# Local attention on one Trainium2 core: two heads in zero-padded query blocks, probabilities divided before their transposes, value products that come out transposed

## The chip, the cores and the metric

The kernel runs on one core of one Trainium2 chip. The core has five engines with a queue each: TensorE (PE in the profile; its weight loads are listed apart as PEld), VectorE (DVE), ScalarE (ACT), GpSimd (POOL) and SyncE (SP), which only issues DMAs here. PE reads its operands from SBUF and writes to PSUM, which has eight banks of 128 partitions by 512 float32 values. The metric is the device time of one execution in microseconds (us), lower is better. Times here come from a set of three runs and from one execution that the hardware profiler recorded.

## The reference

The program is a two-layer network over 16 sequences of 512 tokens with 128 features, all in float32. Layer 0 is `x + s * g`: `s` is a gated causal convolution of the normalised input, and `g` is the SiLU of a small transformer of depth 2 with local attention. Layer 1 is again `x + s * g`, with a 16-head attention and a soft mixture of experts. The change touches the local attention alone, which runs 2 x 16 times (depth times sequences), with 8 heads of 64 and a window of 64:

```python
def local_attention(q, k, v):            # q, k, v: b, h=8, n=512, d=64
    w = n // WINDOW                      # 8 windows of 64 queries
    bq = q.reshape(b, h, w, WINDOW, d) * QK_SCALE
    bk, bv = look_around(bk), look_around(bv)     # window w-1 and window w: 128 keys
    sim = einsum('bhwid,bhwjd->bhwij', bq, bk)
    mask = (i < j) | (i > j + WINDOW) | (j == -1)
    sim = where(mask, -finfo.max, sim)
    attn = softmax(sim, axis=-1)
    out = einsum('bhwij,bhwjd->bhwid', attn, bv)
...
q, k = l2norm(q) * qs, l2norm(k) * ksc
q, k = rotary_xpos(q, k)
o = local_attention(q, k, v)
x = x + o @ wo
```

So each head and window makes a 64 x 128 block of scores, a softmax along its 128 keys, and a 64 x 64 block of output.

## The kernel before

The kernel is written as Python generators, one for each stage and sequence: `conv` (the convolution), `layer(b, 0)` and `layer(b, 1)` (the two depths of the transformer, `L0` and `L0b` in the plan), `pre` (`A`: the second layer norm, projections and rotation of layer 1), `first` and `second` (`S1`, `S2`: the two passes of the 16-head attention, first the row maxima, then the exponentials and value products), and `moe` (`M`). A heap resumes the generators by planned times: every `yield` carries a weight, and a stage's position advances by its weight over the stage's total (`PLAN`, `TOT`). This decides the order in which instructions are recorded. A scheduler then reorders them on each engine by its own timing model (`TLS = True`), taking an instruction that was recorded later where an earlier one is not ready, as far as buffers allow. The order of every engine's queue is therefore fixed when the kernel is built, and on the chip each queue runs strictly in that order, apart from weight loads that PE pulls ahead.

Because several sequences are in flight at once, `L0` of one sequence, `L0b` of the one before, and `A`, `S1`, `S2` and `M` of still earlier ones share the engines. PSUM is divided among them by tags with one bank each: `sc` for scores, `x` and `y` for all other products of `L0` and `L0b`, `pq` for the projections, `a` for the small stages, and `s1`, `s2`, `pv` for the passes of layer 1. Near the end of the program the table `TAIL` lets the last sequences use the banks that have become free.

Inside `layer`, the 8 heads are taken as 4 pairs, `c` = 0 to 3. For each pair:

- `proj(c)` makes queries, keys and values of all 512 tokens (PE `pq`, lines 212 to 214), copies them out of PSUM on ACT (lines 313, 314), rotates and scales them on DVE and POOL (lines 317 to 337), and keeps the values in `vbuf` and a copy shifted by 64 tokens in `vsbuf`. Both hold 64 value columns and a 65th column of ones per head.
- `turn(c)` transposes queries and keys on PE (`qT`, `kT`, helper line 200), and ACT copies each 128 x 512 result into SBUF (lines 344, 347). Rows 0 to 63 belong to the first head of the pair, rows 64 to 127 to the second.
- `attend(c)` then works head by head (`hh`). Eight products of 64 x 64 queries with 64 x 128 keys fill one bank `sc` (line 361): windows 2p and 2p+1 of one head stand in the upper and lower half of the partitions. DVE adds the mask and finds the row minimum of the negated scores (line 371, four instructions, each with a small instruction that reads the accumulator). ACT takes four exponentials (line 373). PE transposes the four blocks (`prT`, line 200), ACT copies them out (line 376), and eight products of 64 rows of probabilities with the 65 value columns fill `po` (line 380). The 65th column holds the sum of the row, so DVE takes its reciprocal (line 387) and multiplies it in on the way out of PSUM (line 388) into `o`. When both heads are done, PE transposes `o` (`oT`, four transposes) and ACT copies the result into the tile `B` (line 391), the stationary operand of the output product (line 404).

After the four pairs come the output product, the residual, the second norm and the gated MLP (lines 404 to 443). In `second`, the four value products of one key tile (line 569) write to four groups of 32 columns of the PE array and are bound together by `behind`, a dependency that keeps their order.

A float32 product appears in the profile as two matrix instructions; a transpose and a product of the rounded type fp32r appear as one. The profile names the part of the PE array that an instruction uses, such as 64\*64 for `sc`, 128\*64 for `po`, 128\*32 for `pvd` and 128\*128 for most others.

## Time and profile before

| | |
|---|---|
| three runs | 3595.16, 3603.40, 3610.21 us; median 3603.4 us |
| profiled execution, its own time | 3609.49 us |
| span of that profile | 3607.5 us |
| mean granted TensorE clock | 0.954 |
| DMA, mean | 63 GB/s |

Span is the time from the first to the last instruction of the core. An engine's busy time is the union of the intervals of its instructions, so overlapping instructions are counted once; the mean duration beside it is that of a single instruction from its start to its end, the overlap included. For pipelined instructions the distance from start to start is therefore shorter than the mean, and it is this distance that the engine's throughput follows. Idle time of an engine is put down to what ended it: another engine's instruction, a DMA, or "issue", where nothing is seen to be waited for. The program can be cut into three stretches: up to 86 us before the first scores of the local attention; from there to the last scores at 3108.6 us; and the end, in which only the later stages of the last sequences are left.

### The profile page before, as it was taken

How to read it: one execution, taken by the hardware profiler on the slowest of the kernel's cores; microseconds unless marked ns; L12 is line 12 of the kernel's file. 1: busy time of each engine (PE TensorE's matmuls, PEld its weight loads, DVE VectorE, ACT ScalarE, POOL GpSimd, SP SyncE). 2: the span in 40 equal slices, each digit the busy share in tenths (PEclk: the TensorE clock that was granted, in tenths of full speed). 3: DMA queues.
4: the chain of work that ended last, by engine and by line, in shares of the span. 5: the costliest groups of instructions: out<-in, count | busy, mean ns of one | idle time of the engine just before them, and what ended most of it. 6: DMA issues, size and time to landing. Idle time of an engine off the chain costs nothing.

```text
span 3607.5 us, 67593 instructions
## 1 busy us (share of the span) xinstructions
PE 3246.8 (90%) x24316; PEld 2324.0 (64%) x24316; DVE 2497.6 (69%) x7065; ACT 2225.3 (62%) x5003; POOL 1677.0 (46%) x1647
## 2 busy tenths in 40 slices
PE   5899878998999999989998999999989998988886
PEld 4788656666766666767675676666767665544542
DVE  7878567677676767777776777767777766654551
ACT  1546545676666666766766676667667665655553
POOL 3234464546464554645655455454645544331310
PEclk7999979899999999999999999999999999999996
DMA  6544441211222212122211212121221211011100
GB/s 220 147 126 113 107 104 43 55 46 44 70 50 58 57 43 62 45 70 50 70 47 47 58 48 66 44 68 44 59 62 44 70 34 53 25 54 40 46 25 13
DMA packets 197723, 227.82 MB, mean 63 GB/s; under 512 B 60016, under 2 KB 125712, under 8 KB 197392
## 3 DMA queue, kind: packets, MB, share of 16 engines
q1 hardware_dynamic: 154384, 138.53, 13.5%
q0 software_dynamic: 43008, 84.97, 9.6%
q8 instruction: 195, 3.19, 0.4%
q14 instruction: 136, 1.11, 0.1%
HBM read 137.49 MB, written 56.10 MB: 54 GB/s over the span
## 4 chain that ended last, share of the span: by engine, by line
PE 52%; DVE 13%; ACT 10%; issue 4%; DMA 2%; POOL 1%; SPq 0%; POOLq 0%; DVEq 0%; ACTq 0%
PE s2d L560 6%; PE pvd L569 6%; PE s1c L533 5%; PE sc L361 5%; DVE mxc L534 3%; PE po L380 3%; ACT sd L562 3%; PE pw L404 2%; PE prT L200 2%; DVE rt L317 2%; DVE q L322 2%; PE pw L442 2%; PE ppb L665 2%; PE pslb L643 1%; PE pq L212 1%
## 5 line engine op out<-in xcount | busy, mean ns | idle before, releaser
L534 DVE TENSOR_REDUCE mxc<-s1c 128x1 f32<-128x512 f32 x1024 | 698.3, 684 | 391.5 <-PE s1c L533 385.2
L562 ACT ACTIVATE sd<-s2d 128x512 f32<-128x512 f32 x1024 | 611.7, 601 | 386.6 <-PE s2d L560 377.5
L330 POOL TENSOR_TENSOR rt<-rt,q 128x512 f32<-128x512 f32 x256 | 333.4, 1303 | 553.4 <-DVE q L322 433.3
L560 PE MATMUL s2d<-QS,KS 128*128 128x512 f32 x1024 | 494.6, 487 | 63.2 <-ACT sd L562 53.8
L533 PE MATMUL s1c<-KS,QS 128*128 128x512 f32 x1024 | 476.1, 466 | 55.5 <-DVE mxc L534 42.8
L373 ACT ACTIVATE s<-s,m 128x128 f32<-128x128 f32 x1024 | 346.4, 397 | 169.5 <-DVE m L371 168.4
L560 PEld LDWEIGHTS s2d<-QS,KS 128*128 128x128 f32 x1024 | 199.0, 195 | 348.4 <-issue 217.4
L336 POOL TENSOR_TENSOR y<-ss,mhalf 128x16 f32<-128x16 f32 x128 | 381.0, 2977 | 64.8 <-DVE ss L334 53.7
L569 PE MATMUL pvd<-sd,Vt 128*32 128x512 f32 x2048 | 286.1, 630 | 29.0 <-ACT sd L562 28.7
L361 PE MATMUL sc<-kT,qT 64*64 64x128 f32 x4096 | 302.9, 281 | 5.9 <-ACT kT L347 2.8
L371 DVE CUSTOM_DVE_ANT_0 s<-sc,maskf 128x128 f32<-128x128 f32 x1024 | 236.3, 284 | 87.8 <-PE sc L361 83.7
L533 PEld LDWEIGHTS s1c<-KS,QS 128*128 128x128 f32 x1024 | 199.6, 195 | 136.8 <-DVE mxc L534 90.0
L313 ACT COPY q<-pq 128x256 f32<-128x256 f32 x512 | 192.3, 376 | 143.9 <-PE pq L214 96.8
L361 PEld LDWEIGHTS sc<-kT,qT 64*64 64x64 f32 x4096 | 228.8, 135 | 77.8 <-issue 22.6
L337 POOL TENSOR_TENSOR rt<-rt,y 128x1024 f32<-128x1024 f32 x128 | 246.6, 1926 | 4.9
L317 DVE TENSOR_TENSOR rt<-q,rot 128x512 f32<-128x512 f32 x256 | 209.0, 820 | 49.9 <-ACT q L313 42.5
L212 PE MATMUL pq<-wq,hT 128*128 128x384 f32 x512 | 212.6, 415 | 31.9 <-ACT vbuf L314 21.5
L200 PE MATMUL prT<-step,s 128*128 128x128 f32 x1024 | 204.0, 288 | 20.3 <-ACT s L373 16.9
L322 DVE TENSOR_TENSOR q<-q,rot 128x512 f32<-128x512 f32 x256 | 216.6, 846 | 4.8 <-ACT q L313 4.7
L545 POOL DMA_DIRECT2D QS<-mxd x128 | 69.1, 541 | 312.2 <-DMA mxd<-sd 273.2
L376 ACT COPY pt<-prT 128x512 f32<-128x512 f32 x256 | 149.3, 583 | 84.2 <-PE prT L200 83.2
L380 PEld LDWEIGHTS po<-vsbuf,pt 128*64 128x64 f32 x2048 | 145.5, 141 | 83.7 <-ACT pt L376 36.7
(246 smaller groups left out, 7654.4 us busy)
## 6 DMA issues: line engine op xcount, KB each, us to landing
wq<-wqd POOLq DMA_DIRECT2D x128, 384.0 KB, 4.0
vsbuf<-vbuf SPq DMA_DIRECT2D x128, 130.0 KB
QS<-scq POOLq DMA_DIRECT2D x128, 128.0 KB, 2.6
KS<-sck POOLq DMA_DIRECT2D x128, 128.0 KB, 2.5
vsbuf<-vbuf SPq DMA_DIRECT2D x128, 97.5 KB
scq<-sa SPq DMA_DIRECT2D x96, 128.0 KB
sck<-sa SPq DMA_DIRECT2D x96, 128.0 KB
toep<-in_wpad_a_dram SPq DMA_DIRECT2D x24, 240.0 KB
```

The lines of the kernel that those rows point to most:

```text
L200: PE.transpose(pt[:, p * 128 : p * 128 + 128], src(p), ident)
L317: V.tensor_tensor(rt[:, ps].rearrange("t p (i h) d -> t p i h d", i=2), qk.rearrange("t p (i h d) -> t p i h d", i=2, h=2), rot[:, l, 0, p ...
L322: V.tensor_tensor(t2, qk.rearrange("t p (i h s d) -> t p i h s d", i=2, h=2, s=2)[:, :, :, :, ::-1, :], rot[:, l, 1, ps].rearrange("t p i ...
L330: G.tensor_tensor(rf, rf, t2.rearrange("t p i h s d -> t (p i h s d)"), ALU.add)
L336: G.tensor_tensor(y.rearrange("t p g -> t (p g)"), ssf, mhalf, ALU.pow)
L361: PE.matmul(s4[q0 : q0 + 64, u // 2, :], qT[r0 : r0 + 64, 64 * u : 64 * u + 64], kT[r0 : r0 + 64, k0 : k0 + 128] if u else kT[r0 : r0 + 64 ...
L373: S.activation(pr[:, p, :], pr[:, p, :], AF.Exp, bias=m[:, p : p + 1], scale=-1.0)
L533: PE.matmul(sc, QS[:, g // 2, qt * 128 : qt * 128 + 128], KS[:, g % 2, :], start=True, stop=True)
L534: V.tensor_reduce(mx[:, g, qt : qt + 1], sc, AX.X, ALU.max)
L560: PE.matmul(sc, KS[:, g % 2, kt * 128 : kt * 128 + 128], QS[:, g // 2, :], start=True, stop=True)
L562: S.activation(e, sc, AF.Exp, scale=ISQ8)
L569: mm = PE.matmul(pv[32 * q : 32 * q + 32, :], Vt[:, kt, 9 * hd : 9 * hd + 32], es[g], start=(kt == 0), stop=(kt == 3),)
```

## The change

The pair of heads is now handled together, and half of the windows at a time.

- `turn` no longer makes a tile `qT`. ACT copies the first head's 64 rows, and DVE the second head's 64 rows, into `qbd`: for each window a 128 x 128 block with the queries of head 0 in the upper left quarter, those of head 1 in the lower right, and zeros elsewhere. The zeros are written once at the start; there is one such tile for each of the two depths.
- `attend` runs over two halves `i` of four windows. A score block is one 128 x 128 product of `qbd` with the 128 keys of both heads, so the partitions of `sc` hold 64 queries of head 0 and 64 of head 1. Four products replace eight.
- The exponential also gives the sum of each row (`accum_out`). DVE takes the reciprocal of the four sums and multiplies the 128 x 512 probabilities by it in SBUF, before the transposes. The columns of ones go.
- In the value products the values are the stationary operand and the transposed probabilities the moving one, so the result has features in partitions and tokens in columns. It is copied straight into `oT` by ACT, 128 x 256 for each half; the tile `o` and the four transposes `oT` go.
- The helper `tied` records all but the first instruction of a group at high priority and chains them with `behind`. It is used for the value products here and, in place of the loop with `behind`, for those of `second`.
- The buffers of the tag `sd` (the exponentials and other tiles of `second`) go from 6 to 5, and those of `qT` and `o` go.

```diff
-    "sd": 6, "ond": 1,
+    "sd": 5, "ond": 1,
...
-        mask[:64, p] = m0 if p == 0 else m
-        mask[64:, p] = m
+        mask[:64, p] = mask[64:, p] = m if p else m0
...
+    def tied(steps):
+        after = None
+        for step in steps:
+            if after is None:
+                after = step()
+                continue
+            with tc.high_priority():
+                mm = step()
+            behind(mm, after)
+            after = mm
...
+        t = wk0.tile([128, 8, 128], F32, name=f"qbd{l}", bufs=1)
+        G.memset(t, 0.0)
+        qbd.append(t)
...
-            v = wk0.tile([128, 4, 2, 65], F32, name=f"vbuf{l}{i}", bufs=1)
-            vs = wk0.tile([128, 4, 2, 65], F32, name=f"vsbuf{l}{i}", bufs=1)
+            v = wk0.tile([128, 4, 2, 64], F32, name=f"vbuf{l}{i}", bufs=1)
+            vs = wk0.tile([128, 4, 2, 64], F32, name=f"vsbuf{l}{i}", bufs=1)
...
-            qT = tl([128, 512], "qT")
-            S.copy(qT, quad(lambda p: rt[:, p, 0:2, :].rearrange("t g d -> t (g d)"), "qT"))
+            qb = qbd[l]
+            pt = quad(lambda p: rt[:, p, 0:2, :].rearrange("t g d -> t (g d)"), "qT").rearrange("d (u q) -> d u q", u=8)
+            S.copy(qb[0:64, :, 0:64], pt[0:64])
+            V.tensor_copy(qb[64:128, :, 64:128], pt[64:128])
...
-            for hh in range(2):
-                r0 = 64 * hh
+            for i in range(2):
...
-                for u in range(8):
-                    q0 = 64 * (u % 2)
+                for w in range(4):
+                    u = 4 * i + w
                     k0 = 64 * max(u - 1, 0)
                     PE.matmul(
-                        s4[q0 : q0 + 64, u // 2, :],
-                        qT[r0 : r0 + 64, 64 * u : 64 * u + 64],
-                        kT[r0 : r0 + 64, k0 : k0 + 128] if u else kT[r0 : r0 + 64, None, 0:64].to_broadcast([64, 2, 64]),
+                        s4[:, w, :], qb[:, u, :],
+                        kT[:, k0 : k0 + 128] if u else kT[:, None, 0:64].to_broadcast([128, 2, 64]),
                         start=True, stop=True,
                     )
...
-                    S.activation(pr[:, p, :], pr[:, p, :], AF.Exp, bias=m[:, p : p + 1], scale=-1.0)
+                    S.activation(pr[:, w, :], pr[:, w, :], AF.Exp, bias=m[:, w : w + 1], scale=-1.0, accum_out=sm[:, w : w + 1])
+                V.reciprocal(sm, sm)
+                V.tensor_tensor(pr, pr, sm[:, :, None].to_broadcast([128, 4, 128]), ALU.mult)
...
-                po3 = pt_("po")[:, 0:260].rearrange("t (p d) -> t p d", p=4)
-                for u in range(8):
-                    PE.matmul(
-                        po3[64 * (u % 2) : 64 * (u % 2) + 64, u // 2, :],
-                        prT[:, 64 * u : 64 * u + 64],
-                        (v if u % 2 else vs)[:, u // 2, hh, :],
-                        start=True, stop=True,
+                po = pt_("po")
+                tied([
+                    partial(
+                        PE.matmul, po[64 * hh : 64 * hh + 64, 64 * w : 64 * w + 64],
+                        (v if w % 2 else vs)[:, 2 * i + w // 2, hh, :], prT[:, w, hh, :], start=True, stop=True,
                     )
-                ri = tl([128, 4], "ri")
-                V.reciprocal(ri, po3[:, :, 64])
-                V.tensor_tensor(o[:, :, hh, :], po3[:, :, 0:64], ri[:, :, None].to_broadcast([128, 4, 64]), ALU.mult)
-                yield 1
-            po = quad(lambda p: o[:, p].rearrange("t h d -> t (h d)"), "oT")
-            S.copy(oT[:, c, :], po)
-            yield 0.8
+                    for w in range(4) for hh in range(2)
+                ])
+                S.copy(oT[:, c, 256 * i : 256 * i + 256], po[:, 0:256])
+                yield 1.4
```

## The prediction

> **What bounds the kernel now.** I read the page's busy shares and granted clock first, then the busy times cut at the last local attention scores (3108.6 us), then the ends of idle time, then the timeline of single groups on PE.
>
> ```profile
> PE 3246.8 (90%) x24316; PEld 2324.0 (64%) x24316; DVE 2497.6 (69%) x7065; ACT 2225.3 (62%) x5003; POOL 1677.0 (46%) x1647
> 86.30:3108.60 3022.30, 2785.01 (x22132) 2061.47 (x22132) 2196.46 (x6341) 1958.32 (x4523) 1528.46 (x1413) 0.97 0.24 63
> 3108.60:3607.50 498.90, 412.52 (x1985) 222.98 (x1981) 237.02 (x500) 251.66 (x446) 119.69 (x191) 0.90 0.13 34
> ```
>
> In the windows (length; busy PE, PEld, DVE, ACT, POOL; clock) PE is busy 92% of the long middle, DVE 73%, ACT 65%. PE is the bound, not a sharp one: busy includes pipeline tails at each wait. In the last 499 us DVE and ACT are at half load: a few dependent streams are left, and time goes into round trips. What is left there:
>
> ```profile
> L562 ACT ACTIVATE sd<-s2d 128x512 f32<-128x512 f32 x259 | 151.1, 598 | 122.9 <-PE s2d L560 117.9 <-DMA mxd<-sd 2.0 <-issue 1.1
> L533 PE MATMUL s1c<-KS,QS 128*128 128x512 f32 x232 | 112.5, 491 | 13.5 <-DVE mxc L534 8.8 <-DMA QS<-scq 2.2 <-DVE rgb L684 0.7
> L569 PE MATMUL pvd<-sd,Vt 128*32 128x512 f32 x520 | 77.7, 673 | 12.4 <-ACT sd L562 12.3
> ```
>
> A sequence has 64 of the first two, so 4.0 and 3.6 sequences of S2 and S1 wait when the local attention ends.
>
> Single groups on PE (start, length, instructions):
>
> ```profile
> 1500.07 0.59 PE L655 MATMUL phb<-sb,wf 128*128 128x512 f32 x1
> 1500.59 0.27 PE L380 MATMUL po<-vsbuf,pt 128*64 128x65 f32 x1
> ...
> 1500.99 0.22 PE L380 MATMUL po<-vbuf,pt 128*64 128x65 f32 x1
> 1501.05 0.22 PE L380 MATMUL po<-vsbuf,pt 128*64 128x65 f32 x1
> 1501.05 0.22 PE L380 MATMUL po<-vbuf,pt 128*64 128x65 f32 x1
> 1501.20 0.38 PE L404 MATMUL pw<-wo,B 128*128 128x128 f32 x1
> 1504.42 1.72 PE L404 MATMUL pw<-wo,B 128*128 128x128 f32 x14
> 1515.32 0.60 PE L200 MATMUL oT<-step,o 128*128 128x128 f32 x4
> 1520.97 0.81 PE L483 MATMUL pya<-wl,sa 128*128 128x384 f32 x2
> 1521.70 1.09 PE L361 MATMUL sc<-kT,qT 64*64 64x128 f32 x16
> 1522.72 0.50 PE L212 MATMUL pg<-hT,w1h 128*128 128x512 f32 x1
> ```
>
> `po` runs two by two, 0.06 us apart, but 0.15 us pass from the last pair to `pw`: leaving a column-split mode costs 0.09. Entering costs as much: `phb` to `po` takes 0.52 us where a full-rate 512-column instruction needs 0.43. Transposes and 128-column instructions follow each other every 0.11 us ((0.60-0.27)/3; (1.72-0.38)/13, with a 128x128 weight load before each, so the loads hide).
>
> **The change part by part.** Counts are those of the built instruction order. My sum is against the profiled execution (3609.5 us, 2.0 around its span), which is 6 us above the median of the three runs.
>
> PE. (1) The 512 `oT` transposes go: 512 x 0.11 = 56 us. (2) The scores leave 64\*64 mode; with fewer split groups, changes of PE mode along the queue fall from 1796 to 1172: 624 x 0.095 = 59 us; at least 2 x 256 groups = 49. (3) A score group took 1.02 us from start to next start, 0.93 without its exit; eight 128\*128 instructions need 8 x 0.11 = 0.88: 256 x 0.05 = 13 us, bounds 0 and 13. (4) `po` keeps 16 instructions, 64 columns for 65, still in alternating halves: 0. Together -128 us. `tied` leaves the number of `pvd` mode changes alone (311 exits before, 313 after): 0.
>
> The Trainium skill speaks against (3): "TensorEngine Tiling (Array Packing)", When to Use Tiling, asks for row tiling where the contraction is 64 or less, and the overview counts four independent tiles of 64x64; padding to 128 gives them up. By that rule a tiled group of eight products of 2 x 0.11 us, four at a time, would take 0.44 us, and the padding would cost 256 x (0.88 - 0.44) = 113 us. The row of 16 instructions in 1.09 us shows only the column pairs overlapping, since a group uses the rows of one head; the measured row decides.
>
> DVE. The multiply by line 388 goes (107.0 us busy). The multiply of 128x512 in SBUF is new: nearest row line 317, 820 ns, also two SBUF inputs; bounds 684 (line 443, one input in PSUM) and 846 (line 322): 256 x 0.82 = 210 us. The copy of 64 rows of `qT`: no such row; partition count does not matter (line 429 takes 743 ns at 85 and at 128), so 128 x 0.684 = 88 us by line 511, bounds 594 (ACT's copy) and 743. Reciprocals stay at 256. Net +191 us (+130 to +205).
>
> The skill's "SBUF — State Buffer", on the shared port pair, says a DVE instruction with two SBUF inputs and a reading GpSimd instruction exclude each other. The trace fits partly: line 317 has 820 ns against 684 with an input in PSUM. At 684 the multiply would be 35 us cheaper.
>
> ACT. `oT`'s copy goes (75.3 us), two of 128x256 come: 256 x 0.376 (line 313) = 96 us, net +21. The row sums add 1024 accumulator reads. The only row like it is in the setup:
>
> ```profile
> 463.53 0.29 ACT L864 ACTIVATE sesq<-se 128x128 f32<-128x128 f32 x1
> 463.73 0.19 ACT L864 ACTIVATION_READ_ACCUMULATOR sesq<-se 128x1 f32 x1
> 463.82 0.29 ACT L864 ACTIVATE sesq<-se 128x128 f32<-128x128 f32 x1
> 464.02 0.19 ACT L864 ACTIVATION_READ_ACCUMULATOR sesq<-se 128x1 f32 x1
> 464.12 0.29 ACT L864 ACTIVATE sesq<-se 128x128 f32<-128x128 f32 x1
> 1710.28 1.28 ACT L373 ACTIVATE s<-s,m 128x128 f32<-128x128 f32 x4 [0.94 <-DVE m L371]
> ```
>
> Starts are 0.29 us apart with a read between, and four exponentials without reads take 1.28 us, also (1.28-0.40)/3 = 0.29 apart. Reads hide inside; I take 0.09 per group of four, 24 us; bounds 0 and 1024 x 0.186 = 190. ACT then stands near 66%.
>
> Queues and buffers. SP keeps 1061 DMA issues and POOL 512; the value shifts shrink by 1/65: 0. Two memsets on POOL at the start: 0, POOL is at 46%. `qbd` has one buffer per depth where `qT` had two, so the next pair's copies wait for the second half's scores; in the order they stand behind them anyway: 0, at worst a 0.6 us hold of ACT's queue 128 times (77 us of idle on an engine with 1000 us of it). `sd` at 5: in both orders one `s2d` stands ahead of each `pvd` group at the end, which five buffers allow: 0.
>
> New waits. First, transposes no longer begin after the first exponential: three more (3 x 0.29), the last read (0.19), a reciprocal (0.17) and the multiply (0.82) come first, about 2 us. PE's queue has, by the distances above, a median 5.7 us of other work between scores and transposes, 3.6 before, so the order makes that room; PE waited 17 us for these over the whole run, I add 25 (0 to 60). Second, DVE goes from 73% to about 82% of the middle, so `s1c`, which waited 43 us for DVE's maxima, waits longer: +25 (0 to 80). The `oT` waits go (from 300 to 3000 us; total, times, longest):
>
> ```profile
> PE s1c L533 <- DVE mxc L534: 33.0, 37, 3.7
> PE oT L200 <- DVE o L388: 13.8, 9, 3.0
> PE prT L200 <- ACT s L373: 13.2, 9, 4.4
> ```
>
> Order of the stages. After the last score group the changed order leaves 155 `s1c`, 189 `s2d` and 192 `pvd` products (before: 232, 259, 260): later stages keep pace with the local attention. The end shrinks: by `s2d` to 499 x 189/259 = 364, by `s1c` to 333; since the last sequence's own chain does not scale, I take 390 (333 to 470). The work that moves into the middle costs PE 77 x 0.23 + 70 x 0.23 + 17 groups x 1.0 = 51 us, and about 31 for the mixture and rotation rows that move along: +82.
>
> Sum: start 86.3 + 2.0 around; middle 3022.3 - 128 + 82 - 15 (`oT` idle) + 50 = 3011; end 390: 3490 us, 3.3% below the profiled 3609.5. As a cross-check, 3609.5 - 128 - 15 with all other waits kept gives 3467.
>
> **The rivals.** A difference of 0.5% (18 us) is about what a measurement of this kernel can tell from no change.
>
> - Half of it: the order's shorter end is paid back in a middle where DVE and ACT stand fuller. New waits of 130 us (nearly the sum of both upper bounds) instead of 50 give 3570; with an end of 360 instead of 390, 3540. For it: 82% on DVE; against: most DVE idle time is waiting for PE.
> - PE's time was not what held it: the removed work turns into idle, and the end does not shrink: 3600. Against: idle on PE in the middle is only 8%.
> - Slower: the reciprocal blocks DVE's queue. It waits for the last exponential; a group of four takes 1.28 us plus up to 0.4 behind the last minimum. Directly behind the minima DVE would stand 1.6 us, 256 x 1.6 = 410 us, and maxima, rotations and bias adds behind it hold PE. In the built order the median is 1.7 us of other DVE work between, but a tenth of the groups have under 0.6. It decides when more than (3609-3490)/256 = 0.47 us per group reaches PE; at 0.7 the time is 3670.
> - The change does not do what it says: weight loads of 128x128 (195 ns) show where 64x64 (135 ns) hid: 2048 x 0.085 = 174 us, 3664. Line 404's spacing speaks against it.
>
> **How the numbers follow.** Main case 0.52; half of it 0.26; no bound 0.08; blocked DVE 0.10; weight loads 0.04. Faster 0.78, same 0.08, slower 0.14. The main case alone spans 3415 (no new waits, end 364) to 3570 (end 470). The range reaches from its low end past the half case up to the no-bound case, 3415 to 3605; the blocked queue and the loads stay outside.
>
> **What will show it.** Right: no 64\*64 score rows and 2048 score instructions 0.11 us apart; PE busy near 3120 us; the last scores near 3100 us and some 390 us behind them; exponentials still 0.29 us apart; transposes waiting little more than 17 us for DVE. Wrong: DVE idle put down to ACT in front of the reciprocal above 120 us, PE waits for DVE beyond 130 us in the middle, or an end still near 500 us.

## The result, and the profile after

The changed kernel takes 3688.12 us (median of 4 runs, 3685.59 to 3690.34) against 3604.14 us for the kernel before (4 runs): ratio 1.0235, 95% interval 1.0212 to 1.0258. It is 2.3% slower; I had forecast 3490 us, 3.3% faster. The execution that was profiled took 3686.83 us with a span of 3685.1 us and a mean granted clock of 0.940 (before: 3609.49, 3607.5 and 0.954).

The busy shares of the page of the changed kernel:

```profile
PE 3172.5 (86%) x21756; PEld 2294.4 (62%) x21756; DVE 2705.7 (73%) x7193; ACT 2333.4 (63%) x6157; POOL 1700.2 (46%) x1641
```

Against before, PE has lost 74 us of busy time, DVE has gained 208 and ACT 108. The same windows as before, cut at the last score group (length; busy PE, PEld, DVE, ACT, POOL with instruction counts; clock, DMA share, GB/s):

```profile
86.90:3328.80 3241.90, 2833.95 (x20149) 2099.48 (x20150) 2482.92 (x6631) 2136.33 (x5796) 1605.02 (x1502) 0.95 0.23 61
3328.80:3685.10 356.30, 290.32 (x1404) 156.49 (x1402) 157.42 (x341) 181.82 (x329) 63.51 (x102) 0.89 0.10 28
```

The end did shrink, from 499 to 356 us. The middle grew from 3022 to 3242 us, and in it PE idles 408 us where it idled 237. Who ended idle time (waits view of the changed kernel, whole run; total us, times, longest; below it the row of the kernel before that answers to the second):

```profile
PEld s1c L542 <- DVE mxc L543: 152.9, 170, 4.5
PE s1c L542 <- DVE mxc L543: 96.9, 88, 4.1
DVE ri L386 <- ACT s L385: 92.2, 71, 5.0
...
PEld kT L212 <- DVE qbd L358: 37.5, 52, 5.8
PE prT L212 <- DVE s L387: 31.3, 40, 3.0
```

```profile
PE s1c L533 <- DVE mxc L534: 42.8, 55, 3.7
```

PE's longest wait is now for DVE's row maxima of `first`: 97 us, where it was 43 over the whole run before. The transposes `prT` wait 31 us for the new multiply. The weight loads of the transposes `kT` stand 38 us behind the new DVE copy into `qbd`: both halves of `qT` have to leave their bank before `kT` is written to it. In the middle as a whole, summed over PE's waits by the engine that ended them, DVE's part went from 93 to 221 us, ACT's from 126 to 152.

The groups (busy us, mean ns | idle before, ended by) that answer the prices of the prediction:

```profile
L373 PE MATMUL sc<-kT,qbd 128*128 128x128 f32 x2048 | 294.0, 287 | 11.8 <-DVE m L383 7.0
L385 ACT ACTIVATE s<-s,m 128x128 f32<-128x128 f32 x1024 | 401.4, 396 | 116.1 <-DVE m L383 112.8
L387 DVE TENSOR_TENSOR s<-s,ri 128x512 f32<-128x512 f32 x256 | 252.0, 984 | 3.6
L385 ACT ACTIVATION_READ_ACCUMULATOR s<-s,m 128x1 f32 x1024 | 196.9, 192 | 0.0
```

The multiply takes 984 ns in the mean, outside my bounds of 684 and 846. The view of that line's instructions (shortest, median and longest in ns) shows that this is a tail and not a longer instruction:

```profile
L387 DVE TENSOR_TENSOR s<-s,ri x256: 630/691/4522, 91.8 to 3332.5; 128x512 f32<-128x512 f32 x128
```

By my count in the timeline, 139 of the 256 multiplies overlap a tensor instruction on POOL and take 1236 ns in the mean, but 691 in the median; the other 117 take 685 in the mean. The row sums, which I had hidden inside the exponentials, in ACT's timeline (start, length; us):

```profile
1717.47 0.40 ACT L385 ACTIVATE s<-s,m 128x128 f32<-128x128 f32 x1 [2.85 <-DVE m L383]
1717.78 0.18 ACT L385 ACTIVATION_READ_ACCUMULATOR s<-s,m 128x1 f32 x1
1717.87 0.39 ACT L385 ACTIVATE s<-s,m 128x128 f32<-128x128 f32 x1
1718.17 0.18 ACT L385 ACTIVATION_READ_ACCUMULATOR s<-s,m 128x1 f32 x1
1718.26 0.38 ACT L385 ACTIVATE s<-s,m 128x128 f32<-128x128 f32 x1
```

With the read in between, exponentials start 0.39 us apart; without it they were 0.29 apart. In the setup row that I had used, 0.29 us held with a read too, but that was another function (a square) with no bias per row. And one score group in PE's timeline:

```profile
2015.49 0.61 PE L373 MATMUL sc<-kT,qbd 128*128 128x128 f32 x4
```

(0.61 - 0.27)/3 = 0.11 us from one score instruction to the next: that price was right.

So there are three candidates for the lost time. **Theory A**: the division ahead (a reciprocal, a multiply, the sums) costs more than PE's saving, either (A1) because it lengthens the chain from scores to transposes, (A2) because the reciprocal stops DVE's queue, or (A3) as plain work on DVE and ACT. **Theory B**: PE's time was not what held the kernel, so that removing 128 us of it brings little. **Theory C**: neither; the built order of this one kernel happens to be a poor one. The experiments take them in turn.

### The profile page after: what moved, and what is told of

Same layout as the page of the kernel before. It is cut to its first block, busy times and chain, and to the rows that moved or that the text cites. A ratio compares the mean times of both kernels' runs of the same rounds, so it can differ in the third digit from the quotient of the medians.

```text
span 3685.1 us, 63631 instructions
## 1 busy us (share of the span) xinstructions
PE 3172.5 (86%) x21756; PEld 2294.4 (62%) x21756; DVE 2705.7 (73%) x7193; ACT 2333.4 (63%) x6157; POOL 1700.2 (46%) x1641
## 4 chain that ended last, share of the span: by engine, by line
PE 49%; DVE 26%; ACT 13%; DMA 5%; issue 4%; POOL 1%; SPq 1%; POOLq 0%; DVEq 0%; ACTq 0%
PE pvd L122 5%; PE s2d L569 5%; PE s1c L542 5%; DVE mxc L543 4%; PE sc L373 3%; DVE q L334 3%; DVE rt L329 3%; PE pw L413 3%; ACT sd L571 3%; ACT s L385 2%; DVE s L387 2%; DVE s L383 2%; PE pw L451 2%; PE prT L212 2%; PE po L125 2%
## 5 line engine op out<-in xcount | busy, mean ns | idle before, releaser
L542 PE MATMUL s1c<-KS,QS 128*128 128x512 f32 x1024 | 484.1, 474 | 113.4 <-DVE mxc L543 96.9
L385 ACT ACTIVATE s<-s,m 128x128 f32<-128x128 f32 x1024 | 401.4, 396 | 116.1 <-DVE m L383 112.8
L122 PE MATMUL pvd<-sd,Vt 128*32 128x512 f32 x512 | 301.0, 673 | 40.8 <-ACT sd L571 40.3
L125 PE MATMUL pvd<-sd,Vt 128*32 128x512 f32 x1536 | 304.4, 673 | 0.0
L373 PE MATMUL sc<-kT,qbd 128*128 128x128 f32 x2048 | 294.0, 287 | 11.8 <-DVE m L383 7.0
L373 PEld LDWEIGHTS sc<-kT,qbd 128*128 128x128 f32 x2048 | 273.4, 200 | 36.3 <-DVE m L383 14.5
L387 DVE TENSOR_TENSOR s<-s,ri 128x512 f32<-128x512 f32 x256 | 252.0, 984 | 3.6
L385 ACT ACTIVATION_READ_ACCUMULATOR s<-s,m 128x1 f32 x1024 | 196.9, 192 | 0.0
```

Source lines behind the costliest of these rows:

```text
L122: after = step()
L125: mm = step()
L373: PE.matmul(s4[:, w, :], qb[:, u, :], kT[:, k0 : k0 + 128] if u else kT[:, None, 0:64].to_broadcast([128, 2, 64]), start=True, stop=True,)
L385: S.activation(pr[:, w, :], pr[:, w, :], AF.Exp, bias=m[:, w : w + 1], scale=-1.0, accum_out=sm[:, w : w + 1])
L387: V.tensor_tensor(pr, pr, sm[:, :, None].to_broadcast([128, 4, 128]), ALU.mult)
L542: PE.matmul(sc, QS[:, g // 2, qt * 128 : qt * 128 + 128], KS[:, g % 2, :], start=True, stop=True)
```

## The experiments

Each number is a median of device time; ratios are against the kernel before on the same chip in the same set, whose median was 3602 to 3607 us. Diffs whose heading says "changed" start from the changed kernel, those that say "before" from the kernel before; of long lines of numbers only the entry that changes is shown. Any edit makes the scheduler build a new order, a point that the last group of runs measures.

### The division, taken out (changed)

```diff
-                V.reciprocal(sm, sm)
-                V.tensor_tensor(pr, pr, sm[:, :, None].to_broadcast([128, 4, 128]), ALU.mult)
```

> The changed kernel with the reciprocal and the multiply of the probabilities left out, so the rows stay undivided (the part of the computation that is missing); everything else, the row sums of the exponentials too, stays. If the division ahead of the transposes is the cause of the loss, in any of its three ways (VectorE time, the reciprocal blocking VectorE's queue, the longer chain from scores to transposes), this goes well below the kernel before: 3490 to 3550 us. If the padding, the VectorE copy of the queries, the reads of the row sums or the binding of groups is the cause, it stays at 3650 us or above.

Measured: 3614.98 us, ratio 1.0028 (1.0006 to 1.0050). Without the two instructions, 256 times each, this build takes 73 us less. That lies between the two ranges expected: the kernel is still no faster than before, though PE's busy time is 103 us below that of before. Page and middle window:

```profile
PE 3143.8 (87%) x21756; PEld 2280.6 (63%) x21756; DVE 2476.4 (69%) x6681; ACT 2320.5 (64%) x6155; POOL 1682.3 (47%) x1641
```

```profile
87.00:3111.90 3024.90, 2692.52 (x19636) 2025.23 (x19637) 2185.62 (x5980) 2057.12 (x5679) 1538.07 (x1425) 0.97 0.24 63
```

PE idles 332 us of the middle, 95 more than before. In this build A has most of the loss, and B is needed for the rest; the last group of runs shows that an order alone can move the changed kernel as far, so the share of A is not settled by it.

### The sums as well (changed)

```diff
-                    S.activation(pr[:, w, :], pr[:, w, :], AF.Exp, bias=m[:, w : w + 1], scale=-1.0, accum_out=sm[:, w : w + 1])
-                V.reciprocal(sm, sm)
-                V.tensor_tensor(pr, pr, sm[:, :, None].to_broadcast([128, 4, 128]), ALU.mult)
+                    S.activation(pr[:, w, :], pr[:, w, :], AF.Exp, bias=m[:, w : w + 1], scale=-1.0)
```

> The changed kernel without the division and without the row sums, so what is left is the padding of the scores, the two copies of the queries and the transposed value products (the division is missing from the result). If the sums on ScalarE were what ate the TensorE time saved in the run without the division alone (3615 us): 3520 to 3570 us. If TensorE's time is worth nothing and ScalarE has room: 3595 to 3620 us.

Measured: 3593.34 us, 0.9962 (0.9944 to 0.9980): 22 us less than with the sums. With all of the division gone, padding, shorter PE work and the transposed result together gain 12 us where PE's own sum said 128.

### Chain, queue or load? (changed)

The first keeps all the work but lets the transposes read the undivided probabilities, so that nothing waits for the multiply; its result goes to a tile that nobody reads. (`kT` gets one buffer instead of two, to make room; also in the next one.)

```diff
-    "kT0": 2,
+    "kT0": 1,
...
+    aside = wk0.tile([128, 4, 128], F32, name="aside", bufs=1)
...
-                V.tensor_tensor(pr, pr, sm[:, :, None].to_broadcast([128, 4, 128]), ALU.mult)
+                V.tensor_tensor(aside, pr, sm[:, :, None].to_broadcast([128, 4, 128]), ALU.mult)
```

> The changed kernel with reciprocal and multiply kept, but the product is written to a tile that nobody reads, and the transposes take the undivided exponentials (so the division is missing from the result); the key tile has one buffer instead of two to make room. VectorE has the same work and still waits for ScalarE at the reciprocal, but the chain from scores to transposes is as short as before. Chain theory: 3500 to 3560 us, close to the run without the division. Load or blocking theory: 3640 to 3700 us, close to the changed kernel.

The second also takes away what the reciprocal waits for: both instructions read operands that are ready early.

```diff
-                V.reciprocal(sm, sm)
-                V.tensor_tensor(pr, pr, sm[:, :, None].to_broadcast([128, 4, 128]), ALU.mult)
+                rc = tl([128, 4], "m")
+                V.reciprocal(rc, m)
+                V.tensor_tensor(aside, rot[:, l, 0].rearrange("t p i d -> t p (i d)"), rc[:, :, None].to_broadcast([128, 4, 128]), ALU.mult)
```

> As the run before it, but reciprocal and multiply take operands that are there early (the row minimum and a constant table), so VectorE has the work without waiting for ScalarE, and the division is missing from the result. Blocking theory: at least 60 us below the run that still waits for ScalarE (its reciprocal sat idle 92 us in the changed kernel). Load theory: no more than 30 us below it, and at least 80 us above the run without the division. Chain theory: within 30 us of both.

Measured: 3682.24 us, 1.0222 (1.0193 to 1.0251), and 3693.13 us, 1.0258 (1.0224 to 1.0292). Neither gives back anything that stands out. In the first, DVE still stops at the reciprocal (groups view):

```profile
L388 DVE TENSOR_TENSOR aside<-s,ri 128x512 f32<-128x512 f32 x256 | 224.7, 878 | 3.6
L387 DVE RECIPROCAL ri<-ri 128x4 f32<-128x4 f32 x256 | 42.9, 168 | 41.7 <-ACT s L386 40.8
```

In the second no such stop can be, and the time is no shorter. In these builds neither A1 nor A2 has anything to give back, which leaves A3: some 220 us of busy time on DVE (2698.7 against 2476.4 without the division), wherever its operands come from. The single `kT` buffer was not tried alone; in the second run's trace PE's score products wait 9 us for the copy of `kT`, against 3 in the changed kernel.

### The same load in the kernel before

The reciprocal and the multiply of the last run, added after the exponentials of the old kernel (line 373), with a single `kT` buffer:

```diff
+                rc = tl([128, 4], "m")
+                V.reciprocal(rc, m)
+                V.tensor_tensor(aside, rot[:, l, 0].rearrange("t p i d -> t p (i d)"), rc[:, :, None].to_broadcast([128, 4, 128]), ALU.mult)
```

> The kernel before with the reciprocal and the 128x512 multiply of early operands into an unread tile added to each head, 256 of each, the same VectorE work as in the changed kernel (and one key buffer instead of two). If VectorE's time is what the loss comes from in any kernel: 3660 to 3700 us, as the same work cost 78 us in the changed kernel. If it costs only together with the other parts of the change: 3600 to 3630 us.

Measured: 3683.39 us, 1.0209 (1.0178 to 1.0241): +78 us, as from the undivided to the loaded changed kernel (3693 - 3615 = 78). On an engine that was busy 69% of the time, 220 us of work that nobody waits for came with a third of themselves in added time, in one build of either kernel. The row sums alone, unused, in the kernel before:

```diff
+                sm = tl([128, 4], "sm")
...
-                    S.activation(pr[:, p, :], pr[:, p, :], AF.Exp, bias=m[:, p : p + 1], scale=-1.0)
+                    S.activation(pr[:, p, :], pr[:, p, :], AF.Exp, bias=m[:, p : p + 1], scale=-1.0, accum_out=sm[:, p : p + 1])
```

> The kernel before with the row sums of the exponentials taken as well and not used: 1024 accumulator reads on ScalarE, which in the changed kernel stretched the distance of two exponentials from 0.29 to 0.39 us, so some 95 us of ScalarE time. If ScalarE's time counts as much as VectorE's (about 0.4 us for each us): 3630 to 3650 us. If it counts fully: 3690 us. If ScalarE has room: 3600 to 3615 us.

Measured: 3672.40 us, 1.0183 (1.0138 to 1.0227): +67 us, three times the 22 us of the changed kernel. So this work has no fixed price; whether the kernel that it is put into or the order of each build makes the difference, these runs do not tell.

### PE's time, up and down (before)

One run makes the `oT` transposes three times (PE +1024 x 0.11 = 113 us), the other leaves out three of every four `prT` and `oT` transposes and copies the fourth block four times, so that PE has 127 us less and all copies, waits and shapes stay; that leaves out part of the computation.

```diff
-            po = quad(lambda p: o[:, p].rearrange("t h d -> t (h d)"), "oT")
+            po = pt_("oT")
+            for _ in range(3):
+                for p in range(4):
+                    PE.transpose(po[:, p * 128 : p * 128 + 128], o[:, p].rearrange("t h d -> t (h d)"), ident)
```

> The kernel before with each of the four oT transposes done three times into the same place, 1024 x 0.11 = 113 us more of TensorE work and nothing else. If TensorE's work sets the pace, as the prediction had it: 3690 to 3720 us. If it does not: 3600 to 3630 us.

```diff
-                S.copy(prT, quad(lambda p: pr[:, p, :], "prT"))
+                pt = pt_("prT")
+                PE.transpose(pt[:, 0:128], pr[:, 3, :], ident)
+                S.copy(prT.rearrange("k (p q) -> k p q", p=4), pt[:, None, 0:128].to_broadcast([128, 4, 128]))
...
-            po = quad(lambda p: o[:, p].rearrange("t h d -> t (h d)"), "oT")
-            S.copy(oT[:, c, :], po)
+            po = pt_("oT")
+            PE.transpose(po[:, 0:128], o[:, 3].rearrange("t h d -> t (h d)"), ident)
+            S.copy(oT[:, c, :].rearrange("k (p q) -> k p q", p=4), po[:, None, 0:128].to_broadcast([128, 4, 128]))
```

> The kernel before with only the last of the four transposes of each prT and oT group done and its block copied to all four places, so 1152 of 1536 of these transposes are missing from the result: 1152 x 0.11 = 127 us less TensorE work, as much as the change was to save, and all else as before. If a microsecond taken from TensorE is worth what an added one costs (77 us for 113): 3510 to 3530 us. If taking is worth less than adding costs, because the other queues then set the pace: 3570 to 3605 us.

Measured: three times 3681.81 us, 1.0206 (1.0172 to 1.0241), +77 us; one of four 3574.91 us, 0.9909 (0.9884 to 0.9935), -32 us. This is the run that my prediction lacked: 127 us taken off PE in the kernel before, with nothing added anywhere, are worth a quarter of themselves, in one build. Its middle:

```profile
86.10:3093.50 3007.40, 2720.80 (x21075) 1974.78 (x21077) 2218.09 (x6364) 1956.76 (x4540) 1534.60 (x1427) 0.95 0.24 64
```

Against before PE has 64 us less busy time in it and the stretch is 15 us shorter; 49 us went into idle time of PE, now 287 us. PE at 92% was not the bound in the sense that its time can be subtracted.

Over the whole run PE's busy time fell by 84 us (3246.8 - 3162.7), not by 127. Most of the rest is the granted clock, which has only two values in the records of these traces, full and half. Two stretches of the changed kernel in which PE was busy throughout with 128-column products show what half is (windows view: length; PE, PEld, DVE, ACT, POOL; clock in the third figure from the end), and ahead of the first stands a wait (timeline):

```profile
1333.50:1336.00 2.50, 2.50 (x14) 2.50 (x13) 1.56 (x3) 1.68 (x6) 0.00 (x0) 0.50 0.00 0
2012.60:2015.20 2.60, 2.60 (x23) 2.60 (x24) 1.14 (x2) 0.50 (x1) 0.00 (x0) 1.00 0.48 156
1332.24 0.51 PE L569 MATMUL s2d<-QS,KS 128*128 128x512 f32 x1 [3.13 <-ACT sd L571]
```

Such products start 213 ns apart at half clock and 112 at full (medians of `ppb` in the changed kernel). PE was busy at half clock for 270 us in the kernel before and 369 us here. By my estimate that adds (369 - 270) x (1 - 112/213) = 47 us to PE's busy time, about what is missing. The clock went to half 32 times in the middle of the kernel before and 52 times here; in the 7 us ahead of a drop PE was busy 65 and 66% of the time (medians), where the median of all stretches of 7 us in the middle is 98 and 96%. So the drops follow stretches in which PE waits; no run tests by itself that the waits bring them about.

### Single parts

The second head's copy into `qbd` on ACT instead of DVE (changed):

```diff
-            V.tensor_copy(qb[64:128, :, 64:128], pt[64:128])
+            S.copy(qb[64:128, :, 64:128], pt[64:128])
```

> The changed kernel with the second head's query copy on ScalarE instead of VectorE, about 88 us of VectorE time moved to ScalarE, which has more room. Load theory: VectorE's added time falls by a quarter to a third, so about 3640 to 3660 us. Chain theory: the copy comes ahead of the scores and takes as long on ScalarE, after the other copy; 3680 to 3700 us. If ScalarE was the tight engine: above 3700 us.

Measured: 3681.05 us, 1.0212 (1.0175 to 1.0249), 7 us less, not the 28 to 48 that the load theory asked for, and within what an order does (below).

The copies of `kT` and `oT` on DVE instead of ACT (before):

```diff
-            S.copy(kT, quad(lambda p: rt[:, p, 2:4, :].rearrange("t g d -> t (g d)"), "kT"))
+            V.tensor_copy(kT, quad(lambda p: rt[:, p, 2:4, :].rearrange("t g d -> t (g d)"), "kT"))
...
-            S.copy(oT[:, c, :], po)
+            V.tensor_copy(oT[:, c, :], po)
```

> The kernel before with the copies of kT and oT out of PSUM on VectorE instead of ScalarE: 152 us off ScalarE, about 175 us onto VectorE. By the prices of added work (ScalarE 0.71 us for each us, VectorE 0.38): 152 x 0.71 = 108 gained, 175 x 0.38 = 67 lost, about 3560 to 3580 us. If taking work off is worth little, only the loss is left: 3650 to 3680 us.

Measured: 3684.58 us, 1.0213 (1.0191 to 1.0234), +77 us. The prices of the added work (67 us for stretched exponentials, 78 for a DVE load) do not add up to a rule by which work could be moved to the cheaper engine.

The padded scores alone (before): `qbd`, its two copies and the loop over halves as in the changed kernel, `sd` 5 and one `kT` buffer; reciprocal, columns of ones, `po` and `oT` as before.

```diff
-            S.copy(qT, quad(lambda p: rt[:, p, 0:2, :].rearrange("t g d -> t (g d)"), "qT"))
+            S.copy(qb[0:64, :, 0:64], pt[0:64])
+            V.tensor_copy(qb[64:128, :, 64:128], pt[64:128])
...
-                        qT[r0 : r0 + 64, 64 * u : 64 * u + 64],
-                        kT[r0 : r0 + 64, k0 : k0 + 128] if u else kT[r0 : r0 + 64, None, 0:64].to_broadcast([64, 2, 64]),
+                        s4[:, w, :], qb[:, u, :],
+                        kT[:, k0 : k0 + 128] if u else kT[:, None, 0:64].to_broadcast([128, 2, 64]),
```

> The kernel before with the padded scores alone: query blocks of two heads with zeros, copied by ScalarE and then VectorE, one buffer of them and of keys, half of the windows at a time; sums by the columns of ones, division after the value products and the oT transposes as before, and five sd buffers. TensorE loses 576 mode changes and 13 us in the scores, 68 us in all; VectorE gains 89 us. By the prices of added work: 3604 - 46 + 34, about 3585 to 3600 us. If TensorE time taken off is worth nothing and the two copies in a row and the single buffer hold the pair up: 3635 to 3680 us.

Measured: 3666.70 us, 1.0167 (1.0144 to 1.0190), +59 us, although PE's busy time falls by 57. Two groups show the new wait (lines by form): the copy on DVE stands 22 us behind ACT's copy of the other 64 rows of the same bank, and the next transposes stand 20 us behind DVE's.

```profile
L348 DVE COPY qbd<-qT 64x512 f32<-64x512 f32 x128 | 88.9, 695 | 25.6 <-ACT qbd L347 22.4
L202 PE MATMUL kT<-step,rt 128*128 128x128 f32 x512 | 82.1, 283 | 20.7 <-DVE qbd L348 20.4
```

That is a part of the 59 us; I have no run that separates the rest, the smaller numbers of `sd` and `kT` buffers among it.

The helper `tied` for both groups of value products, `sd` 5 (before):

```diff
+                tied([
+                    partial(
+                        PE.matmul, po3[64 * (u % 2) : 64 * (u % 2) + 64, u // 2, :],
+                        prT[:, 64 * u : 64 * u + 64], (v if u % 2 else vs)[:, u // 2, hh, :], start=True, stop=True,
+                    )
+                    for u in range(8)
+                ])
...
+                tied(group)
```

> The kernel before with tied for both groups of value products and five sd buffers, nothing else. If the binding or the buffer count is part of the loss: above 3625 us. If not: 3590 to 3615 us.

Measured: 3669.08 us, 1.0163 (1.0136 to 1.0190), +62 us, for an edit without one instruction of the program's own more or less. That cannot be the price of work; it points to C, though the fifth instead of sixth `sd` buffer was not tried alone. The time lies in the end, which takes 553 us instead of 499, with the middle as long as before (3026 against 3022). In the five runs above with a slower kernel before (the DVE load, the row sums, the tripled transposes, the DVE copies, the padding) it is the other way: their middle is 66 to 116 us longer, their end no longer than 499.

### How much is the order?

The plan's times decide the order of recording. I moved one of two of its numbers by less than 1%: `A` from 2.6025 to 2.62, or `L0b` from 1.4137 to 1.42. The program's instructions stay the same; only ACT's table loads, 1.28 us each, follow the order (97 in the changed kernel, 77 under `L0b` 1.42; 95 to 97 in the kernel before).

```diff
-['A', 2.6025, 0.5]
+['A', 2.62, 0.5]
```

> The kernel before with one planned start moved (stage A from 2.6025 to 2.62 of a sequence's period): the same instructions, another order on every engine. Order theory (the kernel before stands at a favourable order that any edit gives up, and the loss of the change is mostly that): 3640 to 3690 us, as much as every kernel measured with added work. Work theory (the added VectorE and ScalarE work is the loss): 3590 to 3620 us.

> The changed kernel with stage A's planned start moved as in the first of these runs. Order theory: the changed kernel has a chance order already, so it moves by up to 30 us in either direction, 3655 to 3715 us, and its mean over orders lies within 30 us of that of the kernel before over orders. Work theory: it stays within 10 us of 3688 us while the kernel before stays near 3604 us.

```diff
-['L0b', 1.4137, 0.98]
+['L0b', 1.42, 0.98]
```

> The kernel before with another planned start moved (stage L0b from 1.4137 to 1.42): the same instructions in another order. Order theory: 3640 to 3690 us again. Work theory: 3590 to 3620 us.

> The changed kernel with stage L0b's planned start moved as in the second of these runs. Order theory: 3655 to 3715 us. Work theory: within 10 us of 3688 us.

And under `L0b` 1.42, `tied` in the kernel before, and `tied` without its high priority in the changed one (`with tc.high_priority()` removed, the chain kept):

> The kernel before with tied groups and five sd buffers, under the plan with L0b at 1.42, to be held against the 3600.5 us of that plan without tied. If binding the groups at high priority costs by itself: 3640 us or above, as under the first plan (3669 us). If the 3669 us was the order of that one build: 3590 to 3620 us.

> The changed kernel under the plan with L0b at 1.42, with its groups chained but without high priority, to be held against the 3612.4 us of that plan with high priority. If high priority costs by itself: 3550 to 3590 us, which would beat both kernels. If it does not: 3600 to 3650 us.

| kernel | plan as it was | `A` 2.62 | `L0b` 1.42 |
|---|---|---|---|
| before | 3604 | 3591.54; 0.9968 (0.9956 to 0.9979) | 3600.54; 1.0000 (0.9983 to 1.0018) |
| changed | 3688; 1.0235 (1.0212 to 1.0258) | 3659.86; 1.0152 (1.0132 to 1.0173) | 3612.40; 1.0028 (1.0015 to 1.0042) |
| before, `tied` | 3669.08; 1.0163 (1.0136 to 1.0190) | | 3625.95; 1.0060 (1.0039 to 1.0080) |
| changed, without high priority | | | 3642.13; 1.0109 (1.0086 to 1.0133) |

Order alone moves the changed kernel over 76 us and the kernel before over 13. So C is right for a large part of the 84 us: under `L0b` 1.42 the changed kernel is 8 us behind the kernel before with its old plan. But under each plan the changed kernel has the longer median, by 84, 68 and 12 us, and in none of these orders does it gain. The 12 us are hardly clear of the scatter: single runs reach from 3603 to 3620 us there, against 3596 to 3614. Neither theory had expected 3612 for the changed kernel (3655 or more, or near 3688). A form of C in which the kernel before owes its time to one lucky order finds no support: both nudges left it as fast or faster. `tied` has no fixed price either: +62 under one plan, +25 under the other; its high priority goes with 30 us less in the changed kernel under `L0b` 1.42. So each of the prices of 59 to 78 us above is that of one build, and how much of it is order is not known.

The windows of the two kernels under `L0b` 1.42, before and then changed:

```profile
86.30:3266.60 3180.30, 2922.72 (x22783) 2124.06 (x22784) 2279.65 (x6514) 2042.01 (x4670) 1592.27 (x1505) 0.97 0.24 63
3266.60:3596.50 329.90, 270.96 (x1333) 147.85 (x1329) 150.89 (x329) 167.19 (x301) 62.47 (x100) 0.90 0.10 26
```

```profile
89.10:3277.40 3188.30, 2814.70 (x20241) 2091.72 (x20242) 2484.07 (x6649) 2125.90 (x5800) 1599.80 (x1504) 0.97 0.24 62
3277.40:3609.20 331.80, 269.24 (x1312) 144.11 (x1310) 148.73 (x323) 166.94 (x304) 62.39 (x100) 0.89 0.10 26
```

This pair is the cleanest comparison of the study: the same end, nearly the same clock, nearly the same instructions behind the last scores. PE is busy 108 us less in the middle, DVE 204 more and ACT 84 more (with 20 table loads, 26 us, fewer over the whole run), and the middle is 8 us longer: PE idles 374 us instead of 258. PE's saving was real and was given back whole as waiting, mostly for DVE: summed by the engine that ended them, PE's waits for DVE in the middle are 203 us instead of 108, those for ACT 132 instead of 129. The row maxima are not where it went in this order (waits view, whole run; changed, then before):

```profile
PE s1c L542 <- DVE mxc L543: 41.6, 67, 3.8
PE prT L212 <- DVE s L387: 34.0, 26, 2.4
PE kT L212 <- DVE qbd L358: 33.7, 52, 5.0
PE sc L373 <- DVE m L383: 19.1, 18, 2.7
```

```profile
PE s1c L533 <- DVE mxc L534: 43.0, 64, 2.3
PE prT L200 <- ACT s L373: 15.8, 17, 4.7
PE kT L200 <- ACT qT L344: 8.4, 16, 0.8
```

The new waits are those for the change's own steps on DVE, the multiply and the copy into `qbd`, and for the row minima behind them. Which waits grow depends on the order; that they are for DVE holds under both plans. It also shows what a shorter end means. The kernel before under this plan has an end of 330 us instead of 499 and takes the same time in all.

The fastest complete kernel of the study is the one before with `A` at 2.62, 0.3% ahead of the kernel before and 2.6% ahead of the changed one (3591.54/3688.12).

## Why the prediction was wrong

The time was 197 us above the forecast in the profiled execution (3686.83 - 3490). By the terms of the sum:

| term | forecast | measured | difference |
|---|---|---|---|
| PE busy, whole program | -128 | -74 | +54 |
| PE busy moved from the end into the middle | 82 | 122 | +40 |
| PE idle in the middle | 237 - 15 + 50 = 272 | 408 | +136 |
| end | 390 | 356 | -34 |

- **The step that failed** is the sum's first: "PE -128", subtracted whole from a middle in which PE was busy 92% of the time. The work was priced right. Scores are 0.11 us apart and their `64*64` rows are gone. Between the two kernels under `L0b` 1.42 PE's busy time differs by 109 us (3242.7 - 3134.0), and PE was busy at half clock for 252 us instead of 210, which by the estimate above took back 20. That it comes off the time was false: 127 us less PE work alone gave 32 us, and under `L0b` 1.42 the middle was 8 us longer with it. My rival "PE's time was not what held it" had the mechanism; I gave it 0.08, with "idle on PE in the middle is only 8%" against it. That 8% measures how full PE was, not what sets the pace, and I had no row for the second. The rival's other half, an end that does not shrink, did not come.
- **The clock** was no term of the sum. In the changed kernel PE was busy at half clock for 362 us, 270 before; by the same estimate that is 44 of the 54 us by which PE's busy time fell short.
- **New waits, +50.** Mis-sized: 186 us by the sum's own terms (408 - 222, the `oT` waits gone), outside the sum of both bounds (140). Of the two terms, the one for the chain held: transposes wait 31 us for the multiply, where 17 + 25 were forecast. The one for a denser DVE did not: `s1c` alone waits 97 instead of 43 us, and 128 us more of PE's idle time in the middle is put down to DVE. The copy into `qbd`, behind which transposes `kT` wait, was no term at all. My bound "PE waits for DVE beyond 130 us in the middle" was crossed, at 221.
- **DVE net +191.** Measured 208 (the lower bound of 130 should have read 144 by its own prices: 256 x 0.684 + 128 x 0.594 - 107). `qbd`'s copy came as priced; the multiply took 984 ns for 820. The small miss is not the failure; giving that work 25 us of new waits was. The same load on its own came with 78 us in a build of either kernel.
- **ACT: "reads hide inside".** Wrong: 0.095 us more per exponential, 1024 x 0.095 = 97 us of ACT where I took 24, inside my bounds (0 to 190). I read the distance from a row of another function. ACT's busy time grew by 108 us against 45 (21 and 24).
- **The end, 390.** Measured 356, nearer than its bounds required, but the inference behind it was false. I took a shorter end as 109 us gained, less 82 for the work moved. Under another plan the kernel before has an end of 330 us and gains nothing. What remains after the last scores tells how the order was cut, not how long the program is.
- **`tied` at 0, buffers and queues at 0.** `tied` with five `sd` buffers changed the time by 25 and by 62 us in the kernel before, by the plan that it was built under. A single built order carries an uncertainty of some tens of us in this kernel, which my range didn't hold. Under `L0b` 1.42 the changed kernel's 3612 us would be 7 us beyond its upper end; so the size of the miss, but not its kind, is in large part one order.
- **The rivals.** "The reciprocal blocks DVE's queue" had the nearest time, 3670, but its sign of 120 us of DVE idle was not reached (92), and the run without that wait was no faster: a number that was near for a wrong reason. "Half of it" named 130 us of new waits, nearer to the 186 that came than my 50, but set them against a PE saving counted in full. The weight loads hid, as the 0.11 us shows.

The Trainium skill's "TensorEngine Tiling (Array Packing)", When to Use Tiling, had spoken against the padding, with 113 us on PE by my estimate from it. The row of 0.11 us per score speaks against that reading here, and the padded scores alone took 57 us off PE's busy time; of the 59 us that they cost in all, the waits named there are a part.

Open: why the changed kernel spreads over 76 us with the order and the old one over 13; which part of the 59 us of padding alone is the wait of one copy behind the other; and what the division costs under the plan with `L0b` 1.42, since it was only taken out under the first. That the lower clock comes from PE's waits is likely by the traces, but not tested; it does not decide the sign, since the run with fewer transposes had the same 0.940 as the changed kernel and was the fastest with the old structure.

## What to carry to other kernels

An engine that is busy 92% of a stretch is not for that reason its bound: before a saving on it is counted, take some of its work away and add some, and read what each direction is worth, and do the same for the engine that gets the new work, even at 70%. Where a scheduler builds the order, build several orders of both versions (here by moving one planned time by less than 1%) before a difference under 2% is put down to an edit. Look at the granted clock in the same step: here part of the work saved on PE came back as half clock. Take the pace of an instruction from rows of its own form; the same read of an accumulator was free behind one function and made another a third longer.

## What the runs showed of the hardware that I had not expected

- A 128x128 exponential with a bias per row and a row sum starts every 0.39 us on ACT, without the sum every 0.29; a square with the sum, in the setup, also every 0.29.
- The granted clock of PE had two values, full and half, with 128-column products 112 and 213 ns apart. With 127 us less PE work it stood at half for longer (369 us of busy time instead of 270).
- A 128x512 multiply with both inputs in SBUF took 685 ns in the mean when no POOL tensor instruction overlapped it and 1236 when one did (691 in the median, 4522 at the longest). This fits what "SBUF — State Buffer" of the Trainium skill (Who interferes with whom) says of the port pair that a DVE instruction with two SBUF inputs and a reading GpSimd instruction exclude each other from; that it is the cause was not tested by a run of its own.
- Two engines that copy different partitions of one PSUM bank into one tile ran one after the other, by a semaphore that the build sets (no run shows what the chip would allow): DVE's copy was held 16 us in all in the changed kernel, 22 us in the one with padding alone (lines by form of the changed kernel):

```profile
L358 DVE COPY qbd<-qT 64x512 f32<-64x512 f32 x128 | 88.9, 694 | 19.9 <-ACT qbd L357 16.3
```
